# Four graph layers on one core: the last layer's 2 × 2 block products by seven products, merged in PSUM by TensorE and ScalarE, with a new order of work

## The chip, the core and the metric

The kernel runs on one core of one Trainium2 chip. The metric is device time in microseconds of one execution; the time of the kernel is the median of several executions. Everything is computed in fp32. TensorE (PE) multiplies, VectorE (DVE), ScalarE (ACT) and GpSimd (POOL) do the elementwise work, SyncE (SP) issues nearly all the DMA transfers. TensorE writes its products to PSUM, which has 8 banks of 128 partitions × 512 fp32 values. VectorE and ScalarE read and write PSUM; GpSimd works in SBUF.

## The reference

The input x is 64 graphs × 256 nodes × 128 features, with one symmetric 0/1 adjacency matrix adj of 256 × 256 that all share. Four layers follow each other, each of the form x = layernorm(x + layer(x, adj)):

```python
# layer 0: attention with row sums u1, u2 of h = x @ others_weight; softmax over the nodes; att @ h + x @ self_weight
# layer 1: h = x @ W; attn = softmax(leaky_relu(h @ a_src + (h @ a_dst)^T) where adj or the diagonal); elu(attn @ h)
# layer 2, five times (a gated unit, in_matrix = out_matrix = adj):
m = adj @ h;  av = concat(m, m)
z = sigmoid(av @ w3.T + w3_b + h @ u3.T + u3_b);  r = sigmoid(av @ w4.T + w4_b + h @ u3.T + u3_b)
hv = tanh(av @ w5.T + w5_b + (r * h) @ u5.T + u5_b)
h = (1 - z) * h + z * hv
# layer 3 (adj0 = adj1 = adj): parts = x, adj x, adj^2 x, adj^3 x, adj x, adj^2 x, adj^3 x
y = sum over k of parts[k] @ weight_1[:, :, k]
```

As both chains of layer 3 use the same matrix, its sum is y = x V0 + (A x) V1 + A² (x V2 + (A x) V3), where V0 is weight_1[..., 0] plus the identity (for the residual) and Vk is the sum of weights k and k + 3. The kernel computes A² once, and per graph A x, then the bracket, then the product with A².

## The kernel before

**Units and lanes.** Two graphs make a unit, so there are NU = 32 units. T is 512 (two graphs' nodes), N is 256, P is 128, NC = 2 halves of the nodes and G = 4 blocks of 128 nodes in a unit. Ten lanes each hold the SBUF tiles for one unit in flight; unit u runs on lane u mod 10. layer0 to layer3 (L649, L756, L880, L983) write down a unit's instructions.

**Who sets the order.** Nothing is issued as it is written down. Every instruction is a Task with an engine and an estimated duration in ns (add, L88). Dependencies come from the Cells that it reads and writes. A Cell of PSUM takes a free bank at its first writer and gives it back when its last user has ended. A write with the same group as the one before does not renew the cell's waits, so the columns of a bank can be written one after another. Plan.run (L118) then plays the whole kernel through: whenever an engine is free, it takes among the ready tasks whose banks can be had the one with the smallest key (first, L1077). The key is the unit number times PERIOD plus the task's due time in its unit, less HASTE for a task that works in an already open bank. The due time adds durations and hand-off times (LATENCY) along the dependencies, times PACE (PACE_GATED in layer 2). TAIL and LATE set the keys of the last ten units. The resulting order is what each engine's queue gets, in order; semaphores for the real dependencies are put in by the framework under it, which keeps accesses of two engines to one bank of PSUM apart.

**Seven products for eight.** A 2 × 2 block product needs eight block products; with sums of blocks on both sides, seven are enough. For A x in layers 2 and 3, left_fast (L839) does that: block_sums (L825) makes four sums of node blocks on GpSimd, fast_blocks (L474) has made the sums of adjacency blocks once, seven products of 128 columns go to two banks x and y, and VectorE adds them up (merged, L868).

**The last layer before.** In layer3 (L983) xT and aT are x and A x with features on the partitions. The products with V0 to V3 are eight products of 256 columns (L1004): for each source, graph and half of the nodes one product with the two weight matrices side by side in w3. They go to banks x and y. ScalarE copies the four blocks of the bracket out of PSUM (L1009, L1010), VectorE makes their block sums (L833 to L836, through block_sums), and seven products of 128 columns with blocks of A² (a2f) are added in PSUM to the other halves or set beside them (L1015). One ScalarE copy (L1028) and five VectorE sums (L1034, merged, L1038) give the output, which goes to layernorm. The last three units (PLAIN = 3) take layer3_end (L1042) instead, with plain products for the end of the run.

**The gates.** Each of layer 2's five steps has five products of 512 columns (L902) into the banks ps_g and ps_v, three tanh on ScalarE (L914, L922, L931) and four elementwise operations on VectorE (L917, L929, L933, L935).

The softmax here doesn't subtract the row's maximum and nothing guards it: scores larger than these inputs give would overflow.

## Time and profile before

| | |
|---|---|
| time, median of 3 (lowest, highest) | 1390.01 us (1389.57, 1390.16) |
| span of the profiled execution | 1387.4 us |
| eight products of 256 columns, L1004 | 464 instructions, 124.0 us busy |
| seven products with A², L1015 | 406 instructions, 56.8 us busy |
| copies of the last layer, L1009, L1010, L1028 | 29 each; 371, 370, 265 ns |
| block sums of the last layer on VectorE, L833, L835, L836 | 29 each; 455, 384, 319 ns |
| sums at its end, L1034, L875, L877, L878, L1038 | 29 each; 413, 413, 283, 414, 278 ns |
| GpSimd sums L833, L835 in gated steps (e<-ht) | 121 each; 862, 596 ns |
| DMA | 147.13 MB, mean 106 GB/s |

The page gives for each engine the time in which it had an instruction under way and its share of the span. Matmul records overlap, so an engine can be busy while short stalls hide in them; the distance from one start to the next is the safer measure. A group of instructions is named by line, engine, output and inputs; a fused fp32 product shows up as two matmul instructions. "<-" names what ended an idle time.

### The profile page before, as it was taken

The numbers are of one execution on the slowest core, as the hardware profiler recorded it, in microseconds if no ns is written. First come the engines' busy times: TensorE is split into PE (matmuls) and PEld (weight loads), VectorE is DVE, ScalarE is ACT, GpSimd is POOL, SyncE is SP. The second block draws the span as 40 slices with busy tenths as digits, with TensorE's granted clock in tenths as the row PEclk, the third lists the DMA queues.
The fourth block names the chain that finished last, engine by engine and source line by source line (L and its number), as shares of the span: only waits on it lengthen the run. The fifth ranks groups of instructions, "written<-read, shape, count | busy, mean of one in ns | idle before, by whom it ended". The sixth has DMA issues, their size and how long they took to land.

```text
span 1387.4 us, 23294 instructions
## 1 busy us (share of the span) xinstructions
PE 1379.3 (99%) x6891; PEld 966.9 (70%) x6891; DVE 1195.8 (86%) x2745; ACT 943.7 (68%) x2303; POOL 629.9 (45%) x1039
## 2 busy tenths in 40 slices
PE   9999999999999999999999999999999999999998
PEld 9776666766676766676766777777666666667777
DVE  6978999998888898888988798899888888998865
ACT  5887656666766777766677678887766655565544
POOL 4234343534355454455354454465443533536433
PEclk9999999999999999999999999999999999999999
DMA  4224545454555555554545554545454454554322
GB/s 129 38 47 103 113 106 106 109 128 111 113 121 107 108 123 105 120 115 104 119 109 115 116 119 115 110 110 121 107 128 100 104 108 95 112 124 115 82 65 61
DMA packets 530077, 147.13 MB, mean 106 GB/s; under 512 B 456480, under 2 KB 495136, under 8 KB 529952
## 3 DMA queue, kind: packets, MB, share of 16 engines
q1 hardware_dynamic: 529152, 145.13, 47.0%
q8 instruction: 55, 0.90, 0.3%
q14 instruction: 70, 0.57, 0.2%
q10 hardware_dynamic: 800, 0.52, 0.1%
HBM read 81.10 MB, written 64.46 MB: 105 GB/s over the span
## 4 chain that ended last, share of the span: by engine, by line
PE 91%; DVE 6%; ACT 1%; issue 1%; POOL 1%; DMA 0%; SPq 0%; POOLq 0%; DVEq 0%; ACTq 0%
PE ps L902 45%; PE ps L844 19%; PE ps L1004 7%; PE ps L743 4%; PE ps L780 4%; PE ps L1015 3%; PE ps L738 2%; PE ps L667 2%; PE ps L792 2%; PE ps L821 1%; PE ps L1051 1%; DVE p L933 1%; DVE st L587 1%; DVE p L546 0%; DVE e L917 0%
## 5 line engine op out<-in xcount | busy, mean ns | idle before, releaser
L902 PE MATMUL ps<-m,gT 128*128 128x512 f32 x960 | 478.6, 593 | 0.0
L902 PEld LDWEIGHTS ps<-m,gT 128*128 128x128 f32 x960 | 166.1, 191 | 113.0 <-issue 91.5
L833 POOL TENSOR_TENSOR e<-ht 128x256 f32<-128x256 f32 x121 | 104.3, 862 | 210.1 <-DMA ht<-hb 153.5
L844 PEld LDWEIGHTS ps<-adjTp,ht 128*128 128x128 f32 x726 | 124.0, 191 | 82.7 <-issue 73.3
L914 ACT ACTIVATE e<-ps,bias 128x512 f32<-128x512 f32 x160 | 109.9, 687 | 95.0 <-PE ps L902 88.4
L931 ACT ACTIVATE p<-ps,bias 128x512 f32<-128x512 f32 x160 | 109.7, 686 | 85.2 <-PE ps L902 83.9
L902 PE MATMUL ps<-e,u5T 128*128 128x512 f32 x320 | 163.2, 593 | 0.0
L592 POOL TENSOR_TENSOR rstd<-ve,nhalf 128x4 f32<-128x4 f32 x126 | 143.6, 1141 | 34.8 <-DVE ve L589 29.8
L589 POOL TENSOR_SCALAR ve<-st 128x4 f32<-128x4 f32 x110 | 38.4, 349 | 259.3 <-DVE st L587 231.3
L844 PE MATMUL ps<-adjTp,e 128*128 128x128 f32 x968 | 149.6, 275 | 0.0
L922 ACT ACTIVATE e<-ps,bias 128x512 f32<-128x512 f32 x160 | 109.8, 688 | 55.5 <-PE ps L902 55.2
L844 PEld LDWEIGHTS ps<-adjTp,e 128*128 128x128 f32 x968 | 130.5, 192 | 13.8 <-issue 11.1
L844 PE MATMUL ps<-adjTp,ht 128*128 128x128 f32 x726 | 138.9, 275 | 0.3 <-DMA ht<-hb 0.2
L933 DVE SCALAR_TENSOR_TENSOR p<-e,p 128x512 f32<-128x512 f32 x160 | 115.2, 721 | 19.4 <-ACT p L931 19.1
L902 PEld LDWEIGHTS ps<-e,u5T 128*128 128x128 f32 x320 | 58.9, 190 | 63.8 <-issue 49.0
L611 ACT ACTIVATE x<-ht,ve,rstd 128x128 f32<-128x128 f32 x212 | 92.4, 489 | 14.3 <-POOL ve L600 14.2
L902 PE MATMUL ps<-xT,gT 128*128 128x512 f32 x192 | 98.0, 593 | 0.0
L875 DVE TENSOR_TENSOR m<-ps,m 128x256 f32<-128x256 f32 x182 | 75.0, 412 | 18.5 <-PE ps L844 17.3
L833 POOL TENSOR_TENSOR e<-x 128x256 f32<-128x256 f32 x61 | 48.7, 798 | 91.8 <-ACT x L611 78.5
L769 ACT ACTIVATE e<-m,esd 128x256 f32<-128x256 f32 x116 | 84.3, 767 | 0.5 <-DMA m<-row 0.5
L917 DVE SCALAR_TENSOR_TENSOR e<-e,xT 128x512 f32<-128x512 f32 x96 | 68.6, 715 | 16.4 <-ACT e L914 15.6
L844 PEld LDWEIGHTS ps<-adjT,x 128*128 128x128 f32 x366 | 60.7, 191 | 29.2 <-issue 24.8
(211 smaller groups left out, 3201.9 us busy)
## 6 DMA issues: line engine op xcount, KB each, us to landing
hb<-p SPq DMA_DIRECT2D x182, 256.0 KB, 2.3
ht<-hb SPq DMA_DIRECT2D x484, 64.0 KB, 2.5
xT<-hb SPq DMA_DIRECT2D x244, 64.0 KB, 2.5
m<-row SPq DMA_DIRECT2D x58, 256.0 KB, 3.7
hb<-p SPq DMA_DIRECT2D x124, 64.0 KB, 1.8
ht<-hb SPq DMA_DIRECT2D x31, 256.0 KB, 2.8
out_dram<-x SPq DMA_DIRECT2D x30, 256.0 KB, 2.5
m<-in_x_dram SPq DMA_DIRECT2D x88, 64.0 KB, 2.4
```

The lines of the kernel that those rows point to most:

```text
L592: add(POOL, 1150, lambda: nc.gpsimd.tensor_tensor(rstd.ap, ve.ap, nhalf.ap, op=ALU.pow), (ve, nhalf), (rstd,))
L611: add(ACT, 400, lambda j=j, b=b, ch=ch, view=view, at=at, shift=shift, col=col: nc.scalar.activation(X[u].ap[:, b, ch, :], view()[:, j, :] ...
L769: add(ACT, 660 if u >= DIRECT_ROWS else 360, lambda g=g, b=b: nc.scalar.activation(e.ap[:, g, :].rearrange("p (c n) -> p c n", c=NC), ev() ...
L833: add(by, wide, lambda: eng.tensor_sub(four[:, 0:2], blk(slice(2, 3)).to_broadcast([P, 2, D]), blk(slice(0, 4, 3))), (src,), (s,), group=ss)
L844: add(PE, mm_ns(P) + 4, lambda: nc.tensor.matmul(ps.ap[:, at * P : (at + 1) * P], lhs(), mat.ap[:, k, c * P : (c + 1) * P], start=start, s ...
L875: add(DVE, 335, lambda: nc.vector.tensor_tensor(mv[:, 1:3], pv(y)[:, 0:2], mv[:, 3:4].to_broadcast([P, 2, P]), op=ALU.add), (y, m), (m,))
L902: add(PE, mm_ns(T), lambda: nc.tensor.matmul(ps.ap, w(), rhs.ap, start=start, stop=stop, skip_group_check=True), (c, rhs), (ps,), after)
L914: add(ACT, 590, lambda ps_g=ps_g, up=up: nc.scalar.activation(r.ap, ps_g.ap, AF.Tanh, bias=bias2.ap[:, 1:2], scale=0.5 / up), (ps_g, bias2 ...
L922: add(ACT, 590, lambda ps_g=ps_g, up=up: nc.scalar.activation(z.ap, ps_g.ap, AF.Tanh, bias=bias2.ap[:, 0:1], scale=0.5 / up), (ps_g, bias2 ...
L931: add(ACT, 590, lambda ps_v=ps_v, up=up: nc.scalar.activation(v.ap, ps_v.ap, AF.Tanh, bias=bias2.ap[:, 2:3], scale=1 / up), (ps_v, bias2), ...
L933: add(DVE, 650, lambda: nc.vector.scalar_tensor_tensor(v.ap, z.ap, 1.0, v.ap, op0=ALU.add, op1=ALU.mult), (v, z), (v,))
L1004: add(PE, mm_ns(N), lambda k=k, src=src, c=c, b=b, ps=ps, at=at: nc.tensor.matmul(gd(ps.ap)[:, at], bn(src.ap)[:, b, c * P : (c + 1) * P], ...
```

## The change

There are three parts.

*The last layer's first products* are seen as a 2 × 2 block product too: rows are the two graphs, the inner blocks are x and A x, columns are the bracket's and the direct part's weights. layer3_blocks makes four sums of halves on GpSimd, and fast_blocks makes the sums of the weight blocks once (w3f). Seven pairs of products of 128 columns take the place of eight products of 256.

*The merging* is moved into PSUM. A partial sum that two results need is accumulated in bank x; ScalarE copies it to slots of bank y, and later products are accumulated onto it there, or on top of it in x. VectorE only makes sums with something kept in SBUF. The block sums of the bracket go from VectorE to GpSimd. Since an accumulating product adds only where PSUM's accumulation bits are set, bank y must be one whose whole width an earlier product has filled: the plan keeps account of that (full, seeded, fits, take).

*The order.* Every task that lies between the taking and the last use of the same bank (hold, within) gets HASTE now, on all engines and 45000 instead of 10000; the pace, hand-off times and tail change, and durations of some VectorE operations in the plan are raised to 575, 655 and 680 ns. Elsewhere in the diff left_fast returns the task that the next product is to follow, and layer3_end finds the halves of w3 exchanged.

```diff
-TAIL = 0.3
+TAIL = 0.2
 LATE = 6
-PACE = 3.0
-PACE_GATED = 1.65
+PACE = 2.5
...
-HASTE = {"pe": 10000.0, "act": 10000.0, "dve": 10000.0}
+HASTE = {"pe": 45000.0, "act": 45000.0, "dve": 45000.0, "pool": 45000.0, "sp": 45000.0}
...
-    LATENCY = {"pe": 500, "dve": 400, "act": 400, "pool": 500, "sp": 3500}
+    LATENCY = {"pe": 400, "dve": 350, "act": 350, "pool": 500, "sp": 4000}
...
+    def fits(self, t):
+        seeded = sum(c.seeded for c in t.takes)
+        return len(t.takes) <= len(self.free_banks) and seeded <= sum(self.full[id(b)] for b in self.free_banks)
+
+    def take(self, t):
+
+        for c in sorted(t.takes, key=lambda c: not c.seeded):
+            c.ap = min(self.free_banks, key=lambda b: self.full[id(b)] != c.seeded)
+            self.free_banks = [b for b in self.free_banks if b is not c.ap]
+
+    def hold(self, tasks):
+
+        bits = {}
+        for t in tasks:
+            own = 0
+            for c in t.banks:
+                own |= bits.setdefault(id(c), 1 << len(bits))
+            t.after = t.before = own
+        for t in tasks:
+            for d in t.deps:
+                if d.unit == t.unit:
+                    t.after |= d.after
+        for t in reversed(tasks):
+            for d in t.deps:
+                if d.unit == t.unit:
+                    d.before |= t.before
+        for t in tasks:
+            t.within = bool(t.after & t.before) and not t.takes
...
+                self.hold(self.tasks[seen:])
...
+                        self.full[id(c.ap)] = c.full
...
-    def bank():
-        return Cell(bank=True)
+    def bank(full=False):
+        return Cell(bank=True, full=full)
+
+    def seeded_bank():
+
+        return Cell(bank=True, seeded=True, full=True)
...
+        c["q"] = Cell(c["r"].ap[:, 2 * P : 4 * P], over=[c["e"], c["r"], c["ex"]])
+        for name, at in (("U", 0), ("p1", 2 * P)):
+            c[name] = Cell(c["z"].ap[:, at : at + 2 * P], over=[c["e"], c["z"]])
...
-    w3 = cell("w3", [D, 2, 2, D])
-    add(POOL, 480, lambda: nc.gpsimd.tensor_add(w3.ap[:, 0, 1, :], wk.ap[:, :, 0], ident.ap), (wk, ident), (w3,))
+    w3f, base = blocks("w3")
+    w3 = Cell(base.ap.rearrange("p k (h d) -> p k h d", h=2))
+    add(POOL, 480, lambda: nc.gpsimd.tensor_add(w3.ap[:, 0, 0, :], wk.ap[:, :, 0], ident.ap), (wk, ident), (w3,))
...
+    fast_blocks(w3f, w3)
...
-            ps_g, ps_v = bank(), bank()
+            ps_g, ps_v = bank(True), bank(True)
...
-        x, y = bank(), bank()
-        home = {(0, 0): (x, slice(0, 2)), (1, 1): (x, slice(2, 4)), (0, 1): (y, slice(0, 3, 2)), (1, 0): (y, slice(1, 4, 2))}
-        for k, src in enumerate((xT, aT)):
-            for (b, c), (ps, at) in home.items():
-                add(PE, mm_ns(N), lambda k=k, src=src, c=c, b=b, ps=ps, at=at: nc.tensor.matmul(
-                    gd(ps.ap)[:, at], bn(src.ap)[:, b, c * P : (c + 1) * P], w3.ap[:, k],
-                    start=(k == 0 and b == 0), stop=(k == 1), skip_group_check=True), (src, w3), (ps,), tail)
-        four, sv = gd(L["xT1"].ap), gd(s.ap)
-        copies = object()
-        add(ACT, 270, lambda: nc.scalar.copy(sv[:, 0:4:3], gd(x.ap)[:, 0:3:2]), (x,), (s,), group=copies)
-        add(ACT, 270, lambda: nc.scalar.copy(sv[:, 1:3], gd(y.ap)[:, 0:2]), (y,), (s,), group=copies)
-        block_sums(s, lambda g: sv[:, g], L["xT1"], -1 in BY_POOL)
-        t, p1, out = L["xT1"], L["v"], L["ht"]
-
-        def one(ps, at, lhs, c, k, start, after=()):
-            return add(PE, mm_ns(P) + 4, lambda: nc.tensor.matmul(
-                ps.ap[:, at * P : (at + 1) * P], a2f.ap[:, k // NC, k % NC * P : (k % NC + 1) * P], lhs(), start=start,
-                stop=True, skip_group_check=True), (c, a2f), (ps,), after, group=four)
-
-        def d(g):
-            return lambda: sv[:, g]
-
-        def sm(k):
-            return lambda: four[:, k]
-
-
-        done = [one(x, 1, d(1), s, 2, False)]
-        one(x, 0, d(0), s, 0, True, done)
-        add(ACT, 160, lambda: nc.scalar.copy(p1.ap[:, 0:P], x.ap[:, 0:P]), (x,), (p1,))
-        done = [one(y, 3, d(3), s, 7, False), one(y, 2, sm(3), t, 3, False)]
-        one(y, 1, sm(0), t, 6, True, done)
-        one(y, 0, sm(1), t, 4, True, done)
-        one(x, 2, sm(2), t, 5, True, done)
-        mv = gd(out.ap)
-        add(DVE, 335, lambda: nc.vector.tensor_tensor(
-            mv[:, 0:4:3], gd(x.ap)[:, 1:3], p1.ap[:, 0:P].rearrange("p (o n) -> p o n", o=1).to_broadcast([P, 2, P]), op=ALU.add),
-            (x, p1), (out,))
-        merged(y, out, None)
-        add(DVE, 200, lambda: nc.vector.tensor_add(mv[:, 3:4], gd(x.ap)[:, 3:4], mv[:, 3:4]), (x, out), (out,))
+        layer3_blocks(u, L, xT, aT, tail)
...
+    def layer3_blocks(u, L, xT, aT, tail):
+        p1, up, sa, sb_, four, out, direct = (L[name] for name in ("p1", "U", "v", "xT1", "m", "ht", "x"))
+        mv, q = L["r"], L["q"]
+        E, f, o = gd2(L["e"].ap), gd2(four.ap), gd2(out.ap)
+        D4 = gd2(direct.ap.rearrange("p b c d -> p (b c d)"))
+        group, ds, es = object(), object(), object()
+
+        def halves(t):
+            return t.ap[:, 0:N], t.ap[:, N : 2 * N]
+
+        x0, x1 = halves(xT)
+        a0, a1 = halves(aT)
+        sums = [*halves(sa), *halves(sb_)]
+        for k, (cell_, i, op, j, cells) in enumerate((
+                (sa, x1, ALU.subtract, x0, (xT,)), (sa, x1, ALU.subtract, a1, (xT, aT)),
+                (sb_, sums[1], ALU.subtract, x0, (sa, xT)), (sb_, sums[2], ALU.add, a0, (sb_, aT)))):
+            add(POOL, 800, lambda k=k, i=i, op=op, j=j: nc.gpsimd.tensor_tensor(sums[k], i, j, op=op), cells, (cell_,), group=group)
+        late = sb_.writers[-2:-1]
+
+        def part(ps, at, n=1):
+            return gd2(ps.ap)[:, at : at + n]
+
+        def one(ps, at, l, cells, r, after=(), start=False, opens=()):
+            def fn():
+                nc.tensor.matmul(part(ps, at)[:, 0], l(), r(), start=start, stop=True, skip_group_check=True)
+
+            return add(PE, mm_ns(P) + 4, fn, cells, (ps, *opens), after, group=group)
+
+        def pair(ps, at, src, cell_, k, after=(), start=False, opens=()):
+            w = w3f.ap.rearrange("p k (c n) -> p (k c) n", c=NC)
+            for c in range(NC):
+                one(ps, at + c, lambda c=c: src[:, c * P : (c + 1) * P], (cell_, w3f), lambda: w[:, k], after, start and not c,
+                    () if c else opens)
+
+        def copied(to, ps, at, n, cell_, g):
+            return [add(ACT, 50 + 110 * n, lambda: nc.scalar.copy(to(), part(ps, at, n)), (ps,), (cell_,), group=g)]
+
+        def added(to, n, ps, at, other, cells, cell_, g):
+            return [add(DVE, 65 + 135 * n, lambda: nc.vector.tensor_add(to, part(ps, at, n), other), (ps, *cells), (cell_,), group=g)]
+
+        x, y = bank(), seeded_bank()
+        pair(x, 0, x0, xT, 0, tail, True, (y,))
+        first = copied(lambda y=y: part(y, 0, 2), x, 0, 2, y, group)
+        pair(x, 0, sums[2], sb_, 5, [*first, *late])
+        second = copied(lambda y=y: part(y, 2, 2), x, 0, 2, y, group)
+        pair(x, 2, sums[1], sa, 4)
+        copied(lambda: gd2(p1.ap), x, 2, 2, p1, None)
+        pair(y, 0, a0, aT, 2, first)
+        copied(lambda: D4[:, 0:2], y, 0, 2, direct, ds)
+        pair(x, 0, sums[0], sa, 6, second)
+        held = added(gd2(up.ap), 2, x, 0, gd2(p1.ap), (p1,), up, None)
+        pair(y, 2, sums[3], sb_, 3, second)
+        added(E[:, 0:2], 2, y, 2, gd2(p1.ap), (p1,), mv, es)
+        pair(x, 0, a1, aT, 7, held)
+        copied(lambda: D4[:, 2:4], x, 0, 2, direct, ds)
+
+        fs = object()
+        add(POOL, 800, lambda: nc.gpsimd.tensor_sub(f[:, 0:2], E[:, 4:5].to_broadcast([P, 2, P]), E[:, 0:6:5]), (mv, up), (four,), group=fs)
+        add(POOL, 600, lambda: nc.gpsimd.tensor_sub(f[:, 2:3], f[:, 1:2], E[:, 0:1]), (mv, four), (four,), group=fs)
+        add(POOL, 600, lambda: nc.gpsimd.tensor_add(f[:, 3:4], f[:, 2:3], E[:, 1:2]), (mv, four), (four,), group=fs)
+
+        def square(ps, at, k, cell_, r, after=(), start=False, opens=()):
+            m = a2f.ap.rearrange("p k (c n) -> p (k c) n", c=NC)
+            one(ps, at, lambda: m[:, k], (cell_, a2f), lambda: r, after, start, opens)
+
+        x, y, os_ = bank(), seeded_bank(), object()
+        square(x, 0, 0, mv, E[:, 0], (), True, (y,))
+        first = copied(lambda: part(y, 0), x, 0, 1, y, group)
+        square(x, 0, 5, four, f[:, 2], first)
+        second = copied(lambda: part(y, 1), x, 0, 1, y, group)
+        square(x, 1, 4, four, f[:, 1])
+        add(DVE, 335, lambda: nc.vector.tensor_add(
+            gd2(q.ap), part(x, 1).to_broadcast([P, 2, P]), D4[:, 1:4:2]), (x, direct), (q,))
+        square(y, 0, 2, mv, E[:, 1], first)
+        added(o[:, 0:1], 1, y, 0, D4[:, 0:1], (direct,), out, os_)
+        square(x, 0, 6, four, f[:, 0], second)
+        held = added(o[:, 3:4], 1, x, 0, E[:, 3:4], (q,), out, os_)
+        square(y, 1, 3, four, f[:, 3], second)
+        added(o[:, 1:2], 1, y, 1, E[:, 2:3], (q,), out, os_)
+        square(x, 0, 7, up, E[:, 5], held)
+        added(o[:, 2:3], 1, x, 0, D4[:, 2:3], (direct,), out, os_)
...
-        soon = HASTE.get(t.eng, 0) if t.banks and not t.takes else 0
+        soon = HASTE.get(t.eng, 0) if t.within else 0
```

## The prediction

> **What bounds the kernel now.** I read the page's busy times first, then TensorE's granted clock over the span, then what TensorE waits for, then its timeline.
>
> ```profile
> span 1387.4 us, 23294 instructions
> ...
> PE 1379.3 (99%) x6891; PEld 966.9 (70%) x6891; DVE 1195.8 (86%) x2745; ACT 943.7 (68%) x2303; POOL 629.9 (45%) x1039
> ...
> PEclk9999999999999999999999999999999999999999
> ```
>
> TensorE is busy for all but 8.1 us, at full clock. A busy TensorE need not be a packed one, so I checked the waits of TensorE and its order of work. The waits:
>
> ```profile
> PE ps L351 <- POOL ident masks.py:199: 1.3, 1, 1.3
> PE ps L780 <- DVE p L773: 0.5, 1, 0.5
> ```
>
> The longest is the identity at the start. Short stalls hide in overlapping records, so I measured start to start in the timeline of a stretch with the last layer in it:
>
> ```profile
> start us, us, engine line op out<-in xcount [idle before <-releaser]
> ...
> 1014.84 1.03 PE L1004 MATMUL ps<-w,xT 128*128 128x256 f32 x4
> 1015.70 1.03 PE L1004 MATMUL ps<-w,m 128*128 128x256 f32 x4
> 1016.57 1.03 PE L1004 MATMUL ps<-w,xT 128*128 128x256 f32 x4
> 1017.43 1.03 PE L1004 MATMUL ps<-w,m 128*128 128x256 f32 x4
> 1018.29 0.38 PE L844 MATMUL ps<-adjTp,ht 128*128 128x128 f32 x2
> ...
> 1023.29 1.05 PE L1015 MATMUL ps<-p,a2T 128*128 128x128 f32 x8
> 1024.18 0.39 PE L844 MATMUL ps<-adjTp,ht 128*128 128x128 f32 x2
> ```
>
> Sixteen instructions of 256 columns take 1018.29 − 1014.84 = 3.45 us: 216 ns each. Eight of 128 columns take 1024.18 − 1023.29 = 0.89 us: 111 ns. Each product is two instructions (8 products of L1004 are 16). Over the whole trace the start-to-start times of the matmuls have medians of 112, 216 and 430 ns for 128, 256 and 512 columns, and all that lies above typical values sums to only 11.4 us: 4.4 in the first 40 us, some 6.7 after 100 us, in which 33 gaps of over 30 ns make 3.7 us. So the time is TensorE's columns, plus about 6 us after its last matmul. The chain that ended last says the same:
>
> ```profile
> PE 91%; DVE 6%; ACT 1%; issue 1%; POOL 1%; DMA 0%; SPq 0%; POOLq 0%; DVEq 0%; ACTq 0%
> PE ps L902 45%; PE ps L844 19%; PE ps L1004 7%; PE ps L743 4%; PE ps L780 4%; PE ps L1015 3%; PE ps L738 2%; PE ps L667 2%; PE ps L792 2%; PE ps L821 1%; PE ps L1051 1%; DVE p L933 1%; DVE st L587 1%; DVE p L546 0%; DVE e L917 0%
> ```
>
> L1004, the products that the change cuts into blocks, is 7% of the chain.
>
> **What the Trainium skill says.** "TensorE: Matmul & The Clock Gate", section "Wait — 56ns, not 53.3ns?", puts a fixed cost of about 2.5 ns on each matmul at full clock beside the time of its columns. So cutting a product into narrower ones should be nearly free. The trace agrees in kind: 2 × 111.5 − 216 = 7 ns for each cut instruction. "PSUM — Partial Sum Buffer", section "The four PSUM rules": a ScalarE write leaves the accumulation bits alone, and a matmul without the first flag adds onto it where the bit is set. That is what the seeded banks use; no row of before has it. Its section "PSUM bank collisions raise a hardware error" says that two engines must not touch one bank at once, other columns included. So each copy or sum must end before TensorE writes that bank again, and this is my main doubt. "GPSIMD Engine Reference", section "8. Key points": GpSimd shares its SBUF interfaces with VectorE instructions of two SBUF inputs. The trace agrees: L933 took 0.68 us with no GpSimd work beside it, 0.82 us with GpSimd busy throughout.
>
> **The change part by part.**
>
> 1. *First products.* Per unit: 8 products of 256 columns become 7 pairs of 128 columns. Removed: 16 instructions × 216 ns = 3.45 us. Added: 14 × 2 = 28 instructions × 111.5 ns = 3.12 us. Saved: 0.33 us, on the engine that sets the end. It is done for 32 − 3 = 29 units (L1004 has 464 = 29 × 16 instructions): 464 × 216 − 812 × 111.5 = 100.2 − 90.5 = 9.7 us.
>
> 2. *Second products.* Seven squares of 128 columns replace seven of 128 columns: nothing. The last three units keep their form: nothing.
>
> 3. *VectorE* loses three block sums and five merges (0.455 + 0.384 + 0.319 + 0.413 + 0.413 + 0.283 + 0.414 + 0.278 = 2.96 us by their rows) and gets three sums of two blocks and four of one (3 × 0.413 + 4 × 0.281 = 2.36 us): −0.60 × 29 = −17 us. More GpSimd work (part 5) slows the gate operations at L917, L929, L933 and L935: 4 × 160 instructions × 0.14 us × 12% more of the span with GpSimd busy (160 of 1387 us) = +10 us. About 1189 us in all; hidden under TensorE.
>
> 4. *ScalarE* copied 0.371 + 0.370 + 0.265 = 1.0 us; now five copies of two blocks and two of one: 5 × 0.37 + 2 × 0.265 = 2.38 us. +1.37 × 29 = +40 us, to 984 of some 1380 (71%); the slack of 32% hides it. Four of these copies go to PSUM, which no row shows. "ScalarE: Activation LUTs", section "What ACT_TABLE_LOAD costs", prices an ACTIVATE with constant scale at 186 + 0.833 N ns: 399 ns for 256 columns; the trace has 371 to SBUF. I take 371; 399 would add 4 × 0.03 × 29 = 3 us to an engine with slack.
>
> 5. *GpSimd* gets five operations of 256 columns and two of 128: 5 × 0.862 + 2 × 0.6 = 5.5 us (rows L833, L835). × 29 = +160 us, to 790 (57%). Hidden, but behind them in its queue stand the block sums of gated steps and the powers of the layer norms. The five new setup operations on w3 (about 0.6 us each, as for a2T) come before the first last layer, at 168 us in before: nothing.
>
> 6. *New turns on TensorE.* The merge in PSUM makes first, second and held copies that later products must follow. Those are dependencies the plan sees, so it puts other units' products between. But pairs and squares of one group don't get a dependency on readers of other slots of the bank (add() renews a cell's waits only when the group changes): the product on x after the copy to p1, on y after the copy of its first half, and the two squares after a VectorE sum. So about 4 a unit, 116 turns in all, can meet a wait that the plan didn't see; behind such a product stands all of TensorE's queue. Lower bound 0, since the plan's hand-off times of 350 to 400 ns may cover the reader; upper bound 116 × 0.37 = 43 us, a whole copy each time. Before's gaps averaged 0.11 us; I take one turn in eight with such a gap: 116 / 8 × 0.11 = 1.6 us.
>
> 7. *Banks and latency.* From its first product to its last merge a last layer took 10 to 26 us, median about 16, in two banks: 32 of the 8 × 43 = 344 bank-us a unit has (1390 us / 32 units = 43). Longer chains, taken as two banks and then two more, stay near that, and their ends may come some us later of the 430 us that a lane gives a unit. A seeded bank has to be one that a filled cell left; gates leave ten of those a unit, two are needed: nothing. The constants (pace, latencies, haste for every task between takers and last users of one bank) only reorder; TensorE is full before, so they can gain at most the 6.7 us of mid-run gaps. What they gain or lose of these the trace can't tell: 0. The end, some 6 us from the last matmul on, is the last units' own code: unchanged.
>
> Sum: 1390.0 − 9.7 + 1.6 = 1381.9, rounded to 1382.
>
> **The rivals.**
> *A, packed as before* (0.58): 1380 to 1386, most likely 1382. For it: TensorE without waits, ten units in flight, slack on every other engine.
> *B, the turns stall TensorE* (0.14, slower): one turn in three with a wait of a whole copy, 116 / 3 × 0.37 = 14 us: 1390 − 9.7 + 14 = 1394. Against: the plan has other products in hand. For: a queue in order, and durations of the plan (110 ns a block for ScalarE plus 50) that are below the measured 265.
> *C, part of it is lost* (0.10, no change): GpSimd in order at 57% delays gated sums, or a looser end, some 8 to 10 us: 1389. For: GpSimd already waits 231 us for statistics and 157 us for gathered halves, so its order is loose. Against: it never shows as a releaser of TensorE after the start.
> *D, the new order also fills gaps* (0.18): up to 5 of the 6.7 us, 1390 − 9.7 − 4 = 1376.
>
> **How the numbers follow.** A and D are faster by over 2.8 us (0.2%), with the edge of A near C: faster 0.76, same 0.10, slower 0.14. The range 1375 to 1391 leaves out B and the tip of D.
>
> **What would show it.** Right: TensorE instructions rise by 812 − 464 = 348, to 7239; its busy time falls to about 1370; the 128-column products of the last layer start 111 to 112 ns apart; busy ScalarE near 984, GpSimd near 790, VectorE near 1189. Wrong: TensorE waits on the new copies or sums, excess between starts well over 11 us (B); gated products waiting on GpSimd (C); excess under 7 us (D); cadence of the pairs above 115 ns (step 1).

## The result, and the profile after

The kernel after takes 1403.5 us (median of 4 runs, 1402.2 to 1405.2), against 1389.8 of the kernel before beside it: a ratio of 1.0101 [1.0083, 1.0118]. It is 14 us slower, where 1382 us was forecast, in a range of 1375 to 1391.

Busy time and instructions, from the page of after:

```profile
span 1401.1 us, 24569 instructions
PE 1380.8 (99%) x7239; PEld 971.4 (69%) x7239; DVE 1212.3 (87%) x2716; ACT 971.0 (69%) x2419; POOL 809.8 (58%) x1247
```

TensorE has 348 instructions more, as forecast, and yet its busy time has risen by 1.5 us where it should have fallen by 10. A busy TensorE here is one with an instruction open, not one that is packed. The products themselves are as cheap as expected. Columns of the next view, TensorE's timeline of after: start in us, length in us, then engine, line, operation and tiles.

```profile
412.88 1.05 PE L1071 MATMUL ps<-w,p 128*128 128x128 f32 x8
413.77 0.95 PE L838 MATMUL ps<-wx,xT 128*128 128x129 f32 x7
```

L1071 is the new block product. Eight instructions take 413.77 − 412.88 = 0.89 us, 111 ns each, and 0.44 us for a run of four is the measure to keep in mind.

I split both spans by the start-to-start times of all matmuls: a typical time for each width (111, 216 and 429 ns), and whatever lies above it, the *excess*. Worked out from the two traces, in us:

```
                                 before    after   difference
first matmul starts                 1.4      1.4       0
columns at typical times         1368.7   1358.6     -10.1
excess over typical times          11.4     32.9     +21.5
last matmul's start to span end     5.9      8.3      +2.3
span                             1387.4   1401.1     +13.7
```

So the 10 us of columns were gained, and over 20 us were lost between the products. The chain that ended last, by engine, on the page of after:

```profile
PE 75%; DVE 12%; POOL 4%; ACT 4%; issue 2%; DMA 2%; SPq 0%; DVEq 0%; ACTq 0%; POOLq 0%
```

TensorE was 91% of it before. Now a quarter of the chain runs through the other engines: work that was hidden sets the pace in places. The waits of TensorE (total us, times, longest us) name no single culprit:

```profile
PE ps L949 <- ACT e L960: 2.3, 5, 0.9
PE ps L1071 <- ACT e L1082: 1.7, 2, 1.4
PE ps L391 <- POOL ident masks.py:199: 1.3, 1, 1.3
PE ps L890 <- ACT e L902: 1.0, 1, 1.0
PE ps L1071 <- DVE e L1118: 0.9, 2, 0.6
```

Before, the second longest row was 0.5 us. L1071's rows are the new products; L949 and L890 are gate and graph products that the change does not touch. Gaps of over 30 ns between products make 29.7 us in 165 places after, against 8.7 us in 64 before. By what the program says that each gapped product waits for, I count after: 8.9 us inside a product (its second instruction late), 8.8 in turns of a PSUM bank that the plan was not told of, 6.5 on results that it was told of, the rest without a clear owner. That attribution is mine; three examples show what such gaps look like. The first is a turn that the plan was not told of, in the timeline of after:

```profile
283.16 0.39 PE L890 MATMUL ps<-adjTp,ht 128*128 128x128 f32 x2
283.68 0.38 DVE L1118 TENSOR_TENSOR e<-ps,x 128x256 f32<-128x256 f32 x1
284.12 0.81 PE L1071 MATMUL ps<-m,a2T 128*128 128x128 f32 x4 [0.57 <-DVE e L1118]
284.77 1.02 PE L949 MATMUL ps<-m,gT 128*128 128x512 f32 x2
```

VectorE reads bank x for the sum q (L1118) until 284.06. The next products of that bank stand at the head of TensorE's queue and start at 284.12, after 0.57 us of idle time. They then take 284.77 − 284.12 = 0.65 us in place of 0.44. The second example is a delay that three queues hand on. In GpSimd's timeline of after:

```profile
320.30 0.56 POOL L635 TENSOR_SCALAR ve<-st 128x4 f32<-128x4 f32 x1 [1.91 <-DVE st L633]
...
323.00 0.91 POOL L879 TENSOR_TENSOR e<-ht 128x256 f32<-128x256 f32 x1
323.87 0.65 POOL L646 TENSOR_TENSOR ve<-nm,rstd 128x4 f32<-128x4 f32 x1
```

and in the timelines of ScalarE and TensorE:

```profile
324.55 0.88 ACT L657 ACTIVATE x<-ht,ve,rstd 128x128 f32<-128x128 f32 x2 [2.55 <-POOL ve L646]
325.33 0.36 ACT L1082 COPY ps<-ps 128x256 f32<-128x256 f32 x1
325.63 0.36 ACT L1082 COPY e<-ps 128x256 f32<-128x256 f32 x1
326.05 1.16 PE L1071 MATMUL ps<-w,p 128*128 128x128 f32 x8 [1.38 <-ACT e L1082]
```

A layer norm's last GpSimd step (L646) comes late. ScalarE stands idle for 2.55 us with that layer norm (L657) at the head of its queue; two copies of the last layer are behind it; and TensorE waits 1.38 us for those. On GpSimd the step stands behind a block sum of a gated step (L879, 0.91 us), but the layer norm's first step there (L635) was late already: GpSimd had been idle for 1.91 us, until VectorE's statistics (L633) came. Where VectorE lost that time is seen further down, beside e12. In the third example one of the new sums stands in the way itself. GpSimd, then ScalarE and TensorE:

```profile
364.00 0.53 POOL L635 TENSOR_SCALAR ve<-st 128x4 f32<-128x4 f32 x1
364.50 1.10 POOL L1063 TENSOR_TENSOR p<-p,xT 128x256 f32<-128x256 f32 x1
365.56 1.52 POOL L638 TENSOR_TENSOR rstd<-ve,nhalf 128x4 f32<-128x4 f32 x1
```

```profile
367.11 0.46 ACT L657 ACTIVATE x<-ps,ones,rstd 128x128 f32<-128x128 f32 x1 [1.95 <-POOL rstd L638]
```

```profile
368.31 0.49 PE L890 MATMUL ps<-adjTp,ht 128*128 128x128 f32 x2 [0.82 <-ACT x L657]
```

L1063 is a block sum of the new last layer. It runs between a layer norm's first step and its power (L638); ScalarE waits 1.95 us for the power, and TensorE 0.82 us for ScalarE.

### The profile page after: what moved, and what is told of

It is laid out like the page before. It is cut to its first block, busy times and chain, and to the rows that moved or that the text cites. A ratio compares the mean times of both kernels' runs of the same rounds, so it can differ in the third digit from the quotient of the medians.

```text
span 1401.1 us, 24569 instructions
## 1 busy us (share of the span) xinstructions
PE 1380.8 (99%) x7239; PEld 971.4 (69%) x7239; DVE 1212.3 (87%) x2716; ACT 971.0 (69%) x2419; POOL 809.8 (58%) x1247
## 4 chain that ended last, share of the span: by engine, by line
PE 75%; DVE 12%; POOL 4%; ACT 4%; issue 2%; DMA 2%; SPq 0%; DVEq 0%; ACTq 0%; POOLq 0%
PE ps L949 38%; PE ps L890 15%; PE ps L1071 8%; PE ps L789 3%; PE ps L826 3%; PE ps L784 2%; PE ps L838 2%; PE ps L713 1%; ACT x L657 1%; PE ps L867 1%; POOL rstd L638 1%; DVE p L979 1%; DVE e L963 1%; DVE m L922 1%; POOL e L879 1%
## 5 line engine op out<-in xcount | busy, mean ns | idle before, releaser
L949 PE MATMUL ps<-m,gT 128*128 128x512 f32 x960 | 478.2, 594 | 2.9 <-ACT e L960 2.3
L949 PEld LDWEIGHTS ps<-m,gT 128*128 128x128 f32 x960 | 163.6, 191 | 113.5 <-issue 93.0
L638 POOL TENSOR_TENSOR rstd<-ve,nhalf 128x4 f32<-128x4 f32 x126 | 148.0, 1175 | 35.9 <-DVE ve L635 29.5
L949 PE MATMUL ps<-e,u5T 128*128 128x512 f32 x320 | 163.3, 593 | 0.2 <-DVE e L963 0.2
L879 POOL TENSOR_TENSOR e<-ht 128x256 f32<-128x256 f32 x121 | 109.1, 902 | 92.6 <-DMA ht<-hb 64.5
L635 POOL TENSOR_SCALAR ve<-st 128x4 f32<-128x4 f32 x110 | 38.0, 345 | 214.6 <-DVE st L633 210.2
L890 PEld LDWEIGHTS ps<-adjTp,ht 128*128 128x128 f32 x726 | 117.3, 191 | 54.2 <-issue 41.9
L890 PE MATMUL ps<-adjTp,e 128*128 128x128 f32 x968 | 151.1, 276 | 1.3 <-ACT e L902 1.0
L979 DVE SCALAR_TENSOR_TENSOR p<-e,p 128x512 f32<-128x512 f32 x160 | 121.9, 762 | 33.7 <-ACT p L977 33.2
L890 PEld LDWEIGHTS ps<-adjTp,e 128*128 128x128 f32 x968 | 131.1, 192 | 18.6 <-issue 11.9
L890 PE MATMUL ps<-adjTp,ht 128*128 128x128 f32 x726 | 137.3, 275 | 1.6 <-ACT x L657 0.8
L949 PEld LDWEIGHTS ps<-e,u5T 128*128 128x128 f32 x320 | 58.9, 190 | 66.9 <-issue 51.2
L657 ACT ACTIVATE x<-ht,ve,rstd 128x128 f32<-128x128 f32 x212 | 92.8, 491 | 16.7 <-POOL ve L646 16.5
L949 PE MATMUL ps<-xT,gT 128*128 128x512 f32 x192 | 98.2, 594 | 0.5 <-DVE m L925 0.4
L963 DVE SCALAR_TENSOR_TENSOR e<-e,xT 128x512 f32<-128x512 f32 x96 | 70.4, 733 | 16.2 <-ACT e L960 13.9
L881 POOL TENSOR_TENSOR e<-e,ht 128x128 f32<-128x128 f32 x121 | 76.8, 635 | 4.3
L890 PE MATMUL ps<-adjT,e 128*128 128x128 f32 x488 | 77.2, 276 | 0.5 <-ACT m L905 0.5
```

The source lines that it names most:

```text
L638: add(POOL, 1150, lambda: nc.gpsimd.tensor_tensor(rstd.ap, ve.ap, nhalf.ap, op=ALU.pow), (ve, nhalf), (rstd,))
L657: add(ACT, 400, lambda j=j, b=b, ch=ch, view=view, at=at, shift=shift, col=col: nc.scalar.activation(X[u].ap[:, b, ch, :], view()[:, j, :] ...
L879: add(by, wide, lambda: eng.tensor_sub(four[:, 0:2], blk(slice(2, 3)).to_broadcast([P, 2, D]), blk(slice(0, 4, 3))), (src,), (s,), group=ss)
L890: add(PE, mm_ns(P) + 4, lambda: nc.tensor.matmul(ps.ap[:, at * P : (at + 1) * P], lhs(), mat.ap[:, k, c * P : (c + 1) * P], start=start, s ...
L949: add(PE, mm_ns(T), lambda: nc.tensor.matmul(ps.ap, w(), rhs.ap, start=start, stop=stop, skip_group_check=True), (c, rhs), (ps,), after)
L963: add(DVE, 680, lambda h=h: nc.vector.scalar_tensor_tensor(r.ap, r.ap, 1.0, h.ap, op0=ALU.add, op1=ALU.mult), (r, h), (r,))
```

## The experiments

What could make 21 us between the products? The change has three parts that could: the new turns in PSUM (*turns*, A in the expectations), the larger GpSimd load (*GpSimd*, G), and the constants with which the plan writes the order (*order*; a part of it, the shorter hand-off times, is C). Theories 1 and 2 of the expectations are turns and order, A' and A'' are narrower forms of A, B says that a plan this full slips in any case, and D that after's order was bad by chance. Some numbers below come from the kernel's plan itself: it plays the whole program through in its own durations before writing the order, and the time at which its last task ends is called *the plan's end* (1379.4 for before, 1373.0 for after). Excess and span are of the profiled run, times are medians, and ratios are to the kernel before on the same chip.

### Each part alone: old layer in the new order, new layer in the old

e1 is the kernel before with after's constants, its hold and within, its hand-off times and its durations. e2 is the kernel after with these put back.

```diff
 e1 (on the kernel before)
-PACE = 3.0
-PACE_GATED = 1.65
+PACE = 2.5
+PACE_GATED = 1.8
-HASTE = {"pe": 10000.0, "act": 10000.0, "dve": 10000.0}
+HASTE = {"pe": 45000.0, "act": 45000.0, "dve": 45000.0, "pool": 45000.0, "sp": 45000.0}
...
-        soon = HASTE.get(t.eng, 0) if t.banks and not t.takes else 0
+        soon = HASTE.get(t.eng, 0) if t.within else 0
```

> The last layer of before, with the order of after: its constants (TAIL, PACE, PACE_GATED, HASTE, LATENCY), haste for every task between the taking and the last use of a bank, and the raised durations. Theory 1 (the turns of the new last layer on PSUM banks stall TensorE): those turns are gone, so excess between matmul starts goes back to about 11 us and the time to 1390, at most 1393. Theory 2 (the new order itself stalls TensorE, whatever the last layer): the extra 21 us of excess stay and the 10 us of columns come back on top: 1405 to 1412. Between the two, say 1398, each has a share.

> The new last layer with seeded banks, with the constants, the haste rule and the durations of before. Theory 1: the turns are still there, 1398 to 1405. Theory 2: the order of before fills TensorE, excess about 11 us, 1380 to 1384.

e1: 1401.5 us, ratio 1.0090 [1.0075, 1.0105], excess 22.7. e2: 1404.4 us, ratio 1.0105 [1.0088, 1.0122], excess 39.2, of which 10 in the last 40 us. Each part alone costs 12 to 15 us, and both together 14: they don't add up. The old layer has none of the new turns, copies or sums, and the new order alone doubles its excess, from 11.4 to 22.7. TensorE's waits of e1:

```profile
PE ps L923 <- ACT e L935: 2.5, 3, 1.4
PE ps L865 <- ACT e L877: 1.7, 4, 0.7
```

These are gate and graph products, as in the first row of after. So step 7's "0" for the constants can't stand. But the order isn't all of it, since the new layer in the old order is as slow. There GpSimd's results come late: ScalarE waits 49.3 us in all for the last GpSimd step of layer norms (L657 on L646), against 16.4 us for the same step in before.

### Hand-off times, and a nudge to one constant

e4 puts back only the longer hand-off times; e11 moves PACE by 0.01, which no theory gives a reason to matter.

```diff
 e4
-    LATENCY = {"pe": 400, "dve": 350, "act": 350, "pool": 500, "sp": 4000}
+    LATENCY = {"pe": 500, "dve": 400, "act": 400, "pool": 500, "sp": 3500}
 e11
-PACE = 2.5
+PACE = 2.51
```

> After with the longer hand-off times of before in the plan (LATENCY 500, 400, 400, 500, 3500), turns untold, plan's own end 1380.8. Theory C: with honest hand-offs the chip ends 8 to 11 us after the plan, 1389 to 1392. Theory A: the turns are still untold, and longer hand-offs cover only part of them, 14 to 25 us, 1395 to 1406.

> After with PACE 2.51 instead of 2.50, which gives another order with nearly the same own end of the plan, 1374.1 us against 1373.0, turns untold. Theory A, in all its forms: the chip again ends 16 to 28 us after the plan, a span of 1390 to 1402. If after's own order was a chance (theory D): within 8 to 11 us of the plan, 1382 to 1385.

e4: 1398.5 us, ratio 1.0069 [1.0054, 1.0084]. e11: 1399.6 us, ratio 1.0077 [1.0062, 1.0092]. The hand-off times gain 5 us by the medians and 4 by the ratios, but a nudge without meaning gains 4 and 3: a rewritten order is worth some us either way, and e4 shows no more than that. So single changes to the plan can't be read below about 5 us, and causes have to be sought with the order held fixed, or with many orders compared.

### The turns, told to the plan

e3 tells the plan what the hardware's semaphores will enforce: a task on a bank follows every earlier reader and writer of that bank on another engine, in whatever slot. e5 does it for e2. The new dependencies also enter hold and so the haste.

```diff
             t.deps.update(c.waits)
+            if c.bank:
+                t.deps.update(o for o in (*c.readers, *c.writers) if o.eng != eng)
```

> As after, but the plan is told of the turns: a task that uses a bank depends on every earlier task of another engine on that bank, so that it no longer puts a product at a time at which ScalarE or VectorE still holds the bank. No work is added or removed. Theory 1: TensorE's stalls at the last layer's products (about 9 of the 33 us of excess) and those that follow from them go, 1382 to 1393. Theory 2: only the stalls at those products themselves can go, 1394 to 1403; the gated steps keep theirs.

> The second kernel (new last layer, order of before) with the turns told to the plan as in the third. Theory 1: as the third kernel, well under the second, 1382 to 1393. Theory 2: no different from the second, 1380 to 1384.

e3: 1401.0 us, ratio 1.0086 [1.0070, 1.0101], excess 30.6. e5: 1407.9 us, ratio 1.0136 [1.0120, 1.0151], excess 39.4. Telling the turns alone does not help: e3 gains 2.5 us on after, and e5 loses 3.5 on e2. What it shows is in the plan: with the turns known, and the same constants, the plan's end goes from 1373.0 to 1389.5 us (e3), and from 1385.7 to 1401.8 (e5). After's plan counted on 16 us that are gone once the turns are told. The edit tells every bank turn of the kernel, those of the older graph products too (in left_fast the product on x after the copy to m, for one), so the 16 us are not the new turns' alone.

### The turns, taken away in after's own order

e10 keeps after's order to the letter. Four readers of the disputed banks (the copy to p1, the first copy to D4, the sums q and o[0:1]) read a fixed tile of SBUF instead; engines, sizes and the plan's reads are kept, so these turns are gone. Other turns that the plan is not told of, of the graph products for instance, stay. The last layer's values are not computed in it, nor in e12 and e13.

```diff
-        copied(lambda: gd2(p1.ap), x, 2, 2, p1, None)
+        copied(lambda: gd2(p1.ap), x, 2, 2, p1, None, fixed[:, 0:2])
```

> The queues of every engine in exactly after's order, but the four readers of a unit whose bank a later product meets untold (the copy to p1, the first copy to the direct half, the sum of the second square, the first output sum) read a constant SBUF tile of the same size instead of the PSUM slot, so no product has to wait for them. What is left out: those four values of the last layer are not the reference's. Theory A (untold turns make the gap of 28 us between after's plan and the chip, directly at the products and by what they delay): excess between matmul starts falls from 33 us by 15 to 20, span 1381 to 1387. Theory A' (only the stalls seen at the products themselves): it falls by 9, span 1390 to 1393. Theory C (late hand-offs in an order too tight): at most 3 us, span 1398 or more.

1402.0 us, ratio 1.0097 [1.0080, 1.0114]; excess 31.3 against 32.9. Without the four turns, after's own order gains some 1.5 us (0.6 by the ratios), less than the intervals tell apart. One thing works against the gain: the readers are slower from SBUF. The two copies take 405 and 407 ns in place of 377 and 378, the sum q 510 in place of 416 and o[0:1] 387 in place of 279, 7.5 us of added work over the run. So e10 bounds the turns only roughly. But the 15 to 20 us of theory A did not come: where the turns go, other waits come up, as in the first row of TensorE's waits of e10.

```profile
PE ps L890 <- ACT e L902: 2.1, 4, 1.0
```

L890's waits on L902 were 1.0 us, once, in after; here they are 2.1, four times. The 8.8 us that I attributed to untold turns are thus no measure of what is won without them.

### GpSimd, made light in after's own order

e12 keeps after's order and cuts the seven new GpSimd operations from 256 or 128 columns to 8. e13 adds e10's edit.

```diff
-            add(POOL, 800, lambda k=k, i=i, op=op, j=j: nc.gpsimd.tensor_tensor(sums[k], i, j, op=op), cells, (cell_,), group=group)
+            add(POOL, 800, lambda k=k, i=i, op=op, j=j: nc.gpsimd.tensor_tensor(sums[k][:, 0:8], i[:, 0:8], j[:, 0:8], op=op), cells, (cell_,), group=group)
```

> Every queue in exactly after's order, but the seven new GpSimd sums of a unit touch 8 columns of a block instead of all (5.9 us a unit by the rows of after, some 1.5 to 2 us then). What is left out: most of the block sums, so the last layer's values are not the reference's. Theory G (GpSimd, whose work takes some 840 us where the plan counts 764, falls behind in stretches, hands its results over late, and TensorE waits in the end): excess between matmul starts falls from 33 us by 8 or more, span 1393 or less. Theory A'' (the turns on banks and the hand-offs through ScalarE and VectorE alone): at most 3 us, span 1398 or more.

> Both edits at once in after's order: the small GpSimd sums and the four readers that read SBUF instead of the disputed PSUM slots. What is left out: block sums and four values of the last layer. If turns and late GpSimd cover for each other, each alone gives little and both together give more than the sum of the two: excess down by 12 or more, span 1389 or less. If neither is the cause: at most 4 us, span 1397 or more.

e12: 1391.7 us, ratio 1.0017 [1.0010, 1.0024], excess 22.3. e13: 1390.7 us, ratio 1.0009 [1.0002, 1.0015], excess 21.0. This is the large term: with the order untouched, the length of seven GpSimd operations is worth 1403.5 − 1391.7 = 11.8 us. The two edits add (1.5 + 11.8 is 13.3, and together they give 12.8), so the turns don't hide behind GpSimd. In e13 the four readers are nearer to their old lengths (q 453 ns, o[0:1] 315), and still the turns give only 1.0 us. From the page of e12:

```profile
PE 1376.9 (99%) x7239; PEld 971.4 (70%) x7239; DVE 1189.6 (86%) x2716; ACT 972.5 (70%) x2419; POOL 695.6 (50%) x1247
...
PE 91%; DVE 5%; ACT 1%; issue 1%; DMA 1%; POOL 0%; ACTq 0%; SPq 0%; POOLq 0%; DVEq 0%
```

GpSimd's busy time falls by 114 us, its 4% of the chain is gone, and TensorE is 91% of the chain again. But VectorE's busy time falls as well, by 22.7 us, with its instructions unchanged. Groups by form, after and then e12 (instructions, busy us, mean ns, idle us before them):

```profile
L1063 POOL TENSOR_TENSOR p<-p,xT 128x256 f32<-128x256 f32 x29 | 28.3, 977 | 1.6
L979 DVE SCALAR_TENSOR_TENSOR p<-e,p 128x512 f32<-128x512 f32 x160 | 121.9, 762 | 33.7 <-ACT p L977 33.2
```

```profile
L1063 POOL TENSOR_TENSOR p<-p,xT 128x8 f32<-128x8 f32 x29 | 9.6, 331 | 1.6
L979 DVE SCALAR_TENSOR_TENSOR p<-e,p 128x512 f32<-128x512 f32 x160 | 117.1, 732 | 38.0 <-ACT p L977 37.2
```

The gate operation L979 is untouched by the edit and runs in 732 ns in place of 762. So a GpSimd sum costs twice: in GpSimd's own queue, and in VectorE's operations beside it. e12 changes both at once. But every queue has the same order in after and in e12, so the two traces can be laid side by side. In the second example above, the statistics (L633) stand behind these three VectorE operations; after, then e12:

```profile
315.46 1.21 DVE L975 SCALAR_TENSOR_TENSOR p<-e,xT 128x512 f32<-128x512 f32 x1
316.59 1.21 DVE L858 SCALAR_TENSOR_TENSOR ht<-e,ht 128x512 f32<-128x512 f32 x1
317.83 1.10 DVE L859 TENSOR_TENSOR ht<-ht,x 128x512 f32<-128x512 f32 x1
```

```profile
313.34 0.68 DVE L975 SCALAR_TENSOR_TENSOR p<-e,xT 128x512 f32<-128x512 f32 x1
313.94 0.68 DVE L858 SCALAR_TENSOR_TENSOR ht<-e,ht 128x512 f32<-128x512 f32 x1
314.66 0.69 DVE L859 TENSOR_TENSOR ht<-ht,x 128x512 f32<-128x512 f32 x1
```

In after they run while GpSimd makes the four new sums of the unit (313.53 to 318.38), and take 3.5 us in place of 2.1. From L635 to L646 GpSimd takes as long in e12 as in after, and TensorE's wait is 0.23 us there in place of 1.38. So this delay comes from slowed VectorE operations, while that of the third example, which e12 does not have, comes from a new sum in GpSimd's queue. Over the whole run TensorE loses over 30 ns against e12 in 52 places, 12.8 us together, and makes up 2.2 elsewhere. Followed back by releasers, some 5 us of the 12.8 lead to longer VectorE operations and about as much to GpSimd's queue; the rest has no clear origin. This division is an estimate from the two traces; no run separates the two ways.

### GpSimd's true lengths in the plan

In after, GpSimd's start-to-start times sum to 841 us where the plan has 765; on ScalarE the two agree (925 and 924). If the plan only believed its GpSimd too fast, true durations should mend it.

```diff
-        wide, narrow = (780, 580) if by_pool else (350, 215)
+        wide, narrow = (880, 625) if by_pool else (350, 215)
...
-            add(POOL, 800, ...
+            add(POOL, 905, ...
```

> After with GpSimd's durations in the plan raised to what the trace shows from start to start (sums of two blocks 780 to 880 and 800 to 905, of one block 580 to 625 and 600 to 670, small ones 300 to 400 and 250 to 360, powers 1150 to 1195), turns untold. The plan's own end is 1387.1 with 19.7 us of planned idle time of TensorE, so the order is another one. Theory G: span within 10 us of the plan's end, 1394 to 1397. Theory A'': 15 us or more after it, 1402 or more.

1405.6 us, ratio 1.0118 [1.0103, 1.0133], excess 36.7. That version of the theory falls. As with the turns, the more honest plan ends late (1387.1 in its own time, from 1373.0) under these constants, and the chip ends another 18 us after it. VectorE's lengths in the plan, 1161 us against 1212 busy on the chip, were left as they were; no run raised them.

### Constants chosen again

If honest plans end late under after's constants, other constants may suit them. e6 and e7 are e3 with six constants chosen, among many sets, for the earliest plan's end; e8 is e6 without the turns told; e9 is the old layer with the turns told and constants chosen in the same way.

```diff
 e6 (on e3)
-TAIL = 0.2
-LATE = 6
-PACE = 2.5
-PACE_GATED = 1.8
-HOLD = 80
+TAIL = 0.27
+LATE = 5
+PACE = 2.13
+PACE_GATED = 2.39
+HOLD = 60
...  HASTE 45000 -> 96900 on all engines
 e7: TAIL 0.2, LATE 6, PACE 1.88, PACE_GATED 2.51, HOLD 40, HASTE 34300 on TensorE and 117000 elsewhere
 e9: TAIL 0.19, PACE 2.69, PACE_GATED 2.59, HOLD 100, HASTE 30300 on TensorE and 45000 elsewhere
```

> New last layer, turns told to the plan, and six constants of the order (TAIL, LATE, PACE, PACE_GATED, HOLD, HASTE) chosen so that the plan's own last task ends earliest, at 1372.8 us. So far the span lay above the plan's own end by 8.0 (before, 1379.4), 10.9 (old layer, new order, 1387.8), 9.3 and 3.5 (turns told, 1389.5 and 1401.8), but by 28.1 (after, 1373.0) and 19.4 (new layer, old order, 1385.7), where the new layer's turns are untold. Theory A (untold turns are what the plan gets wrong): plan's end plus 8 to 11, so a span of 1381 to 1384, a time near 1384, faster than before. Theory B (a plan this full slips in any case, by slower engines than it assumes): plus 20 or more, 1393 or above.

> As the run with the six chosen constants, from another start of the choice: other constants (PACE 1.88, PACE_GATED 2.51, LATE 6, TAIL 0.2, HOLD 40, HASTE 34300 for TensorE and 117000 elsewhere), plan's own end 1373.4. Theory A: span 1381 to 1385. Theory B: 1393 or above. It tells whether the outcome hangs on one lucky order.

> The first kernel of this set with the turns no longer told to the plan, all its constants kept. The plan's own end is 1371.3, earlier than with the turns told. Theory A: plan's end plus 20 to 28, a span of 1391 to 1399, slower than the first by 10 us or more though its plan ends 1.5 us sooner. Theory B: no more than 2 us from the first.

> The last layer of before under the same treatment: new order rule, turns told, the six constants chosen for the earliest own end of the plan, 1377.5. Theory A: plus 8 to 11, a span of 1385 to 1389, so that the new last layer's fewer columns show as some 5 us between the two chosen kernels. Theory B: 1395 or above.

```
                                        us    ratio to before            span   excess   plan's end
e6  new layer, turns told, chosen   1383.6    0.9957 [0.9942, 0.9972]   1379.9    12.8    1372.8
e7  the same, another choice        1384.9    0.9971 [0.9960, 0.9983]   1383.9    15.7    1373.4
e8  e6 with the turns untold        1389.0    1.0000 [0.9991, 1.0008]   1387.2    21.3    1371.3
e9  old layer, turns told, chosen   1387.9    0.9989 [0.9981, 0.9998]   1386.7    10.7    1377.5
```

e6 is faster than both kernels, and with a quarter more GpSimd work than before (790 us against 630) it has nearly before's excess. From its page:

```profile
PE 1368.0 (99%) x7239; PEld 969.1 (70%) x7239; DVE 1207.2 (87%) x2716; ACT 976.3 (71%) x2419; POOL 790.4 (57%) x1247
...
PE 94%; DVE 4%; POOL 0%; ACT 0%; issue 0%; DMA 0%; SPq 0%; DVEq 0%; POOLq 0%; ACTq 0%
```

GpSimd is at 790 us, and 0% of the chain: the same sums that cost 11.8 us in after's order appear nowhere in the chain of this one. TensorE's waits of e6, with no row of the new products (L1073 in this kernel) among the longest:

```profile
PE ps L624 <- DVE esd L796: 1.5, 1, 1.5
PE ps L393 <- POOL ident masks.py:199: 1.3, 1, 1.3
PE ps L951 <- DVE e L965: 0.7, 1, 0.7
```

In e8 the turn of the sum q is back at the top of TensorE's waits:

```profile
PE ps L1071 <- DVE e L1118: 1.5, 2, 1.2
```

Three comparisons follow. e8 against after is the same code with other constants: −14.5 us, though the plan's end differs by only 1.7 us. e6 against e8 is the telling of the turns: −5.4 us, about half of what theory A expected, and gaps of over 30 ns fall from 18.1 to 9.7 us; the edit rewrites the order, so by e11 most of this may be luck. e6 and e7 against e9 are new layer against old, each with its own chosen order: 3 to 4 us faster, no more than the nudge of e11 moves.

One pattern runs through all these kernels. The span lies 16 to 28 us above the plan's end where the new layer's turns are untold (after, e2, e4, e8, e11, e14), and 3.5 to 11 us above it where they are told (e3, e5, e6, e7) or where the layer is the old one (before, e1, e9). The stalls at the turns are not what fills that gap: e10, without the four, still ends 26.5 us after its plan.

## Why the prediction was wrong

*Step 1, first products: right.* −9.7 us forecast, −10.1 by typical start-to-start times. *Step 2* and the 7239 instructions: as forecast.

*Step 3, VectorE: undersized, and "hidden under TensorE" wrong.* 1189 us forecast, 1212 measured. Its +10 us for gate operations slowed by GpSimd was too small: beside e12 those four (L963, L975, L979, L981 in after) take 16.4 us more in sum, and operations that the step did not count 9.6 more. The second example shows such slowed operations reaching TensorE. In e1 VectorE's busy time rose too, with the same operations and the old layer: from 1196 to 1209 us.

*Step 4, ScalarE: right.* 971 us against 984; a copy of 256 columns from PSUM to PSUM took 364 ns, so the trace's 371 ns was the better of the two values.

*Step 5, GpSimd: the size right, "hidden" wrong.* This is the largest term shown. 790 us were forecast and 810 measured, but the same order with short sums is 11.8 us faster. The step named what stands behind these sums, the gated block sums and the layer norms' powers, and then put no cost on it; the reason given, under rival C, is that GpSimd never shows as a releaser of TensorE. That is no proof: GpSimd releases ScalarE, and ScalarE's queue releases TensorE. The first of these hand-offs was there to see in ScalarE's waits of before:

```profile
ACT x L611 <- POOL ve L600: 16.4, 20, 2.3
```

For the same step it is 22.9 us in after and 18.6 in e12. Share of the span was the wrong measure; GpSimd can be busy 58% of it and still finish late the one step that a full TensorE needs, or slow the VectorE operations before that step. Nor is the work costly in itself: in e6, in another order, GpSimd (790 us) and VectorE (1207 us) are nearly as busy, ScalarE waits 16.9 us for that step, and the excess is 12.8 us.

*Step 6, turns: as stalls about right, their place in the plan left out.* It forecast 1.6 us of stalls, and by e10 and e13 the four turns cost 1.0 to 1.5 us, within the noise and with slower readers in their place. What the step did not ask is how the order changes when the plan doesn't know them: it promises 1373.0 us, where with all turns told it comes to 1389.5. What the telling is worth on the chip is not shown: e3 gained 2.5 us, e5 lost 3.5, and e6 gained 5.4 on e8.

*Step 7, constants "can gain at most the 6.7 us" and so "0": wrong.* The bound on the gain was sound, but there was none on the loss. The old layer in the new order lost 12 us (e1). "The end ... unchanged" was wrong as well: it is 2.3 us longer. The timeline of after at the end shows it:

```profile
1393.04 1.04 POOL L638 TENSOR_TENSOR rstd<-ve,nhalf 128x4 f32<-128x4 f32 x1
1394.05 1.36 POOL L678 TENSOR_TENSOR rstd<-ve,nhalf 128x2 f32<-128x2 f32 x2
1395.38 0.20 POOL L646 TENSOR_TENSOR ve<-nm,rstd 128x4 f32<-128x4 f32 x1
1396.46 1.25 ACT L657 ACTIVATE x<-ht,ve,rstd 128x128 f32<-128x128 f32 x3
1397.74 0.37 SPq L1129 DMA_DIRECT2D out_dram<-x  x1
```

A late unit with the new layer is still in its layer norm (L638, L646, L657) when the last units need GpSimd for theirs (L678), and its output (L1129) is the last to leave.

Sum of the miss, in span: columns −0.4, end +2.3, excess 21.5 in place of 1.6, +19.9: 21.8 us. Of the excess of 21.5, e12 shows 10.6 us to hang on the length of the GpSimd sums, and e13 some 1.3 more on the four turns. The other 9.6 are not taken apart for the new layer. That the order makes them is argued from e1, where the same constants added 11.3 us of excess to the old layer, and from e8, where other constants took 11.6 us of it from the same code.

The rivals: B came nearest in time (1394), by luck: e10 leaves its mechanism only a small part. C named a part of the right mechanism, GpSimd in order delaying what is behind it, and put 8 to 10 us on it. That this is near the 11.8 measured is luck in part, since about half of the loss goes over slowed VectorE operations by the estimate above; and C lacked the order's share. D hoped that a new order fills gaps; this one opened them.

Two things stay open: how e12's gain divides between late GpSimd results and slowed VectorE operations, which is only estimated, and why the same code loses so much more under after's constants than under e8's when the plan's ends are 2 us apart.

## What to carry to other kernels

Where one engine is full and every order is written ahead, "hidden" must be shown for a queue, not for a share of the span: ask what stands behind the new work in its in-order queue and which operations of other engines it slows, and follow both over two or three hand-offs to the full engine. A plan that is not told of waits that the semaphores will make promises too much; here the chip ended 16 to 28 us after such plans. The constants of an order belong to one set of work: after's cost the same code 14 us against others. So compare old and new code each in an order chosen for it. With an order so sensitive that a constant moved by 0.01 shifts the time by 3 to 4 us, an edit's worth is best measured with the order held fixed; then two traces can also be laid side by side, instruction by instruction.

## What the runs showed of the hardware

A stall costs more than the wait. Of 72 products (two instructions each) that stalled at the first instruction in after, 66 also had their second instruction late, by a median of 102 ns over all such gaps; these make 8.9 of the 29.7 us of gaps. So by this trace a late operand costs its lateness and about 0.1 us more.

VectorE operations with two SBUF inputs slow beside GpSimd's sums. L975, which reads two SBUF tiles, took 0.68 us in e12 and 1.21 in after, where GpSimd ran new sums beside it. The same sum q of 256 columns took at most 426 ns in after, with one input in PSUM. In e10, with both inputs in SBUF, 10 of 29 took 475 to 949 ns, each of them beside block sums on GpSimd; the others took at most 430.

A GpSimd sum of 8 columns (the four of L1063) still takes 252 to 331 ns, against 846 to 977 for 256. ScalarE's copy of 256 columns from PSUM takes 364 ns to PSUM and 377 or 378 to SBUF. "ScalarE: Activation LUTs" of the Trainium skill, section "Step-by-step: what each stage is for", says that a ScalarE result reaches PSUM faster than SBUF. The trace of after agrees by 13 to 14 ns at 256 columns, and not at 128, where copies took 270 ns to PSUM and 267 or 268 to SBUF.
